# Routing the last sequence of a mixture-of-experts layer as a whole, with its small tiles in the attention's buffers

## The chip, the cores and the metric

The kernel runs on one core of one Trainium2 chip. The metric is the time of one execution on the device in microseconds (us), as the median of several runs; lower is better. The profile is that of one further execution, the profiled one, whose own time is given beside its span (first to last instruction). A core has five engines with a queue of instructions each: PE (TensorE, matrix products; PEld is its weight load), DVE (VectorE), ACT (ScalarE), POOL (GpSimd) and SP (SyncE, which here only issues transfers), and 16 DMA engines that all queues share.

## The reference, cut to what matters

The input x is 4 sequences of 1024 tokens with 256 features. Four layers follow one another, each added to x after a layer norm: a recurrent scan, a mixture of 8 experts (2 per token), a causal attention of 16 heads, and a mixture of 32 experts with 4 per token. The change is in the fourth:

```python
scores = jax.nn.sigmoid(X @ gate_w.T)
_, idx = jax.lax.top_k(scores + bias[None, :], K)            # K = 4 of E = 32
w = jnp.take_along_axis(scores, idx, axis=-1)
w = w / jnp.clip(jnp.sum(w, axis=-1, keepdims=True), 1e-12, None)
...
pos = jnp.take_along_axis(jnp.cumsum(onehot, axis=0) - 1, eid[:, None], axis=1)[:, 0]
valid = pos < C                                               # C = 256 places per expert
xe = jnp.zeros((E, C, D), x.dtype).at[eid, posc].add(jnp.where(valid[:, None], Xrep, ...))
h = jax.nn.silu(jnp.einsum('ecd,edi->eci', xe, W1)) * jnp.einsum('ecd,edi->eci', xe, W3)
ye = jnp.einsum('eci,eid->ecd', h, W2)
...
out = yrows.reshape(-1, K, D).sum(axis=1)
out = out + jax.nn.silu(X @ sw1.T) * (X @ sw3.T) @ sw2.T      # the shared expert
```

A place in an expert is given out in the order of the tokens, over all four sequences; who comes after the 256th gets none. So a token's place needs the counts of all tokens before it.

## The kernel before

x stays in SBUF as `x[b]`, one per sequence, [128, 8 tiles, 256 features and 7 further columns]: a tile is 128 tokens. The further columns carry mean, deviation and the slots of a token.

**Route** (`l4_route`, L920–1063) works on half a sequence, 4 tiles: mean and variance per tile (L927, L928), the reciprocal root in small steps on DVE (L895–912), the normalised rows `xn` (L934), their transposes on PE into `pt` (L946) and copies to `xT` by ACT (L950), the gate matmuls `pl` (L952–958, through `mm2`, L914, in two halves of 64 columns). Then on [128, 4 tiles x 32 experts]: score by Exp on ACT (L962) with an add and a reciprocal on DVE (L964, L965), score plus bias `selx` (L970), the best 8 per tile (L975, one instruction per tile), `match_replace` per tile (L980), `mask` (L982); a running count per expert, tile by tile (L986–993), which begins with the last count of the half before (`runs1`); the position of each token in each expert by matmuls `pos` (L998, L999); slot, free and their product (L1003–1007), the slots sorted per tile (L1010), the row numbers (L1013–1018). Each row goes to its slot in DRAM (`xs_d`) by an indirect DMA on POOL (`to_slots`, L874). In the last sequence only those of the best expert are sent at once, one per tile, so 4 per half; the others are kept in the list `late`, for a branch that is taken only when the lists overflow. After that come the shared expert's hidden rows (`s_l` matmuls, tanh L1040, L1041, L1043, each 128x512), the sum of the chosen scores (L1049–1053), and for each of the 4 choices three instructions that give `gates` (L1057, L1060, L1061). The function is a generator: its `yield` marks the places at which it may stop.

**Order of the work.** The attention is written out by hand under `manual_schedule` (`run_steps`), an order that the scheduler keeps. In its gaps `Beside` (L1571–1594) steps through a list of such generators, one piece at a time. Sequences 0 to 2 are routed that way, beside the next sequence's attention. After them comes `l4_experts_beside` (L1153–1245): the first list, up to 12 tiles of expert work, two by two. One round is: load of rows (`room`<-`xs_d`, SP, L1129) and weights (POOL, L1124), row numbers on DVE (L1134–1150), transposes `pta` (L1240), copy (L1242), matmuls `pea` (L918), tanh (L1227), two DVE products (L1228, L1229), matmuls `pya`, copy (L1212), and two scatters to `yt_d` (POOL, L874). What of it is left when the attention ends is done next. Then sequence 3 is routed, half after half:

```python
        drain(l3_out(B - 1, ps_s, "s"))
        while beside.jobs or beside.job is not None:
            beside.step()
        late = []
        for h in range(2):
            drain(l4_route(B - 1, h, sm, ps_s, "s", late))
```

Outside `manual_schedule` the scheduler orders each engine's queue and places waits; the order of issue above is only where it starts from.

**The end** (L1732–1895) opens new pools in the memory that the attention's pools gave back. In the order of the program: the total counts `pn` (L1780, L1781), `taken_b` (L1784), the list of the last 4 tiles (L1094–1114), the flag of an overflow (L1796–1800), 24 loads `yg` of expert results on SP (`l4_take`, L1747: 8 of 512 KB for sequence 0, with all four choices, and 16 of 128 KB for sequences 1 and 2, with the first), the last 4 tiles of expert work (`l4_tiles`: weights `ew` on POOL L1124, rows `xg` on SP L1129, L1134–1150, transposes `ptg` L1816, copy `xgT` L1818, `eh` L1825, `hid` L1830–1832, `ey` L1837, copy L1839, scatter to `yt_d`), the shared expert (`sy`, L1078), 48 adds of `yg` times gate into x (`l4_add`, L1756), stores of each half sequence on ACT's queue (L1774), and last the 8 loads `yg`, 8 adds and 2 stores of sequence 3.

Each DMA queue's completions are counted on 8 semaphores that the scheduler hands out in turn, to the loads of SP and the stores of ACT alike; a transfer waits for the one that had its semaphore before.

Of the kernel before, what the change touches and what calls it, by code (L numbers as in the profile page):

```python
# [57 lines left out]
def block_kernel(  # L58
# [861 lines left out]
    def l4_route(b, h, sm, ps, tag, late=None):  # L920

        nm = f"l4_{b}_{h}"
        HT = NT // 2
        half = slice(h * HT, (h + 1) * HT)
        for i in range(h * HT, (h + 1) * HT):
            st = l4s.tile([P, 6], F32, name=f"st_{nm}_{i}", tag="st1")
            nc.vector.bn_stats(st, x[b][:, i, :D])  # L927
            nc.vector.bn_aggr(x[b][:, i, D : D + 2], st)  # L928
            yield "dve"
        yield from rstd_pieces(x[b][:, half, D + 1], nm)  # L930
        xns = []
        for i in range(h * HT, (h + 1) * HT):
            xn = sm.tile([P, D], F32, name=f"xn_{nm}_{i}", tag="ln_xn", bufs=4)
            nc.vector.tensor_scalar(  # L934
                xn, x[b][:, i, :D], x[b][:, i, D : D + 1], x[b][:, i, D + 1 : D + 2],
                ALU.subtract, ALU.mult,
            )
            xns.append(xn)
            if i % 2:
                yield "dve"  # L940
        xT = l4s.tile([P, NC_, 512], F32, name=f"xT_{nm}", tag="xT1")
        for c in range(NC_):
            yield "pe"
            pt = ps.tile([P, 512], F32, name=f"pt_{nm}_{c}", tag=tag)
            for q in range(HT):
                nc.tensor.transpose(  # L946
                    pt[:, q * P : (q + 1) * P], xns[q][:, c * P : (c + 1) * P], ident
                )
            yield "post"
            nc.scalar.copy(xT[:, c, :], pt)  # L950
        yield "pe"
        pl = ps.tile([P, HT, E1], F32, name=f"pl_{nm}", tag=tag)  # L952
        for q in range(HT):
            for c in range(NC_):
                mm2(
                    pl[:, q, :], xT[:, c, q * P : (q + 1) * P], gate1_t[:, c, :],
                    c == 0, c == NC_ - 1,
                )
        yield "post"

        score = l4s.tile([P, HT, E1], F32, name=f"score_{nm}", tag="score")
        nc.scalar.activation(score, pl, AF.Exp, scale=-1.0)  # L962
        yield "dve"
        nc.vector.tensor_scalar(score, score, 1.0, None, ALU.add)  # L964
        nc.vector.reciprocal(score, score)  # L965
        yield "dve"

        selx = l4s.tile([P, HT, E1 + 8], F32, name=f"selx_{nm}", tag="selx")
        nc.vector.memset(selx[:, :, E1:], LOWEST)
        nc.vector.tensor_add(  # L970
            selx[:, :, :E1], score, bias1_t.unsqueeze(1).to_broadcast([P, HT, E1])
        )
        top = l4s.tile([P, HT, 8], F32, name=f"top_{nm}", tag="top1")
        for q in range(HT):
# [3 lines left out]
        rep = l4s.tile([P, HT, E1 + 8], F32, name=f"rep_{nm}", tag="rep1")  # L978
        for q in range(HT):
            nc.vector.match_replace(rep[:, q, :], top[:, q, :], selx[:, q, :], LOWEST)  # L980
        mask = l4s.tile([P, HT, E1], F32, name=f"mask_{nm}", tag="mask1")
        nc.vector.tensor_scalar(mask, rep[:, :, :E1], LOWEST, None, ALU.is_equal)  # L982
        yield "dve"


        run = l4s.tile([P, HT + 1, E1], F32, name=f"run_{nm}", tag="run1", bufs=2)  # L986
        if runs1:
            nc.vector.tensor_copy(run[:, 0, :], runs1[-1][:, HT, :])
        else:
            nc.vector.memset(run[:, 0, :], 0.0)  # L990
        runs1.append(run)
        for q in range(HT):
            nc.vector.tensor_add(run[:, q + 1, :], run[:, q, :], mask[:, q, :])
        yield "pe"
        pp = ps.tile([P, HT, E1], F32, name=f"pos_{nm}", tag=tag)
        for par in range(2):
            r = slice(par * DH, (par + 1) * DH)
            nc.tensor.matmul(pp[r], lower[:, r], mask, start=True, stop=False)  # L998
            nc.tensor.matmul(pp[r], ones[:, r], run[:, :HT, :], start=False, stop=True)  # L999
        yield "post"  # L1000

        slot = l4s.tile([P, HT, E1], F32, name=f"slot_{nm}", tag="slot1")
        nc.vector.tensor_add(slot, pp, slot1.unsqueeze(1).to_broadcast([P, HT, E1]))  # L1003
        free = l4s.tile([P, HT, E1], F32, name=f"free_{nm}", tag="free1")
# [3 lines left out]
        srt = l4s.tile([P, HT, 8], F32, name=f"srt_{nm}", tag="srt1")  # L1008
        for q in range(HT):
            nc.vector.max(srt[:, q, :], slot[:, q, :])  # L1010
        srt = srt[:, :, :K1]
        yield "dve"
        nc.vector.tensor_copy(x[b][:, half, D + 2 : D + 2 + K1], srt)  # L1013
        none = l4s.tile([P, HT, K1], F32, name=f"none_{nm}", tag="none1")
        nc.vector.tensor_scalar(none, srt, 0.0, float(NSLOT + 1), ALU.is_equal, ALU.mult)
        nc.vector.tensor_add(none, none, srt)
        row = l4s.tile([P, HT, K1], I32, name=f"row_{nm}", tag="row1", bufs=2)
        nc.vector.tensor_scalar(row, none, 1.0, None, ALU.subtract)
        for k in range(K1):
            for q in range(HT):  # L1020
                to = (row[:, q, k : k + 1], x[b][:, h * HT + q, :XP])
# [4 lines left out]
        nc.vector.tensor_reduce(  # L1026
            second[:, 2 * b + h : 2 * b + h + 1], srt[:, :, 1], AX.X, ALU.max
        )


        hid = l4s.tile([P, 512], F32, name=f"sh_{nm}", tag="shid", bufs=2)
        for w in (sw1_t, sw3_t):
            yield "pe"
            pt = ps.tile([P, 512], F32, name=f"s{0 if w is sw1_t else 1}_{nm}", tag=tag)
            for c in range(NC_):
                mm2(pt, w[:, c, :], xT[:, c, :], c == 0, c == NC_ - 1)
            yield "post"

            if w is sw1_t:
                nc.scalar.activation(hid, pt, AF.Tanh, scale=0.5)  # L1040
                nc.vector.scalar_tensor_tensor(hid, hid, 1.0, pt, ALU.add, ALU.mult)  # L1041
            else:
                nc.vector.scalar_tensor_tensor(hid, pt, 0.5, hid, ALU.mult, ALU.mult)  # L1043
        hid1[b, h] = hid


        yield "dve"
        gsum = l4s.tile([P, HT], F32, name=f"gsum_{nm}", tag="gsum1")
# [4 lines left out]
        nc.vector.tensor_mul(score, score, gsum.unsqueeze(2).to_broadcast([P, HT, E1]))  # L1053
        for k in range(K1):
            yield "dve"
            eq = l4s.tile([P, HT, E1], F32, name=f"eq_{nm}_{k}", tag="eq1")
            nc.vector.tensor_tensor(  # L1057
                eq, slot, srt[:, :, k : k + 1].to_broadcast([P, HT, E1]), ALU.is_equal
            )
            nc.vector.tensor_mul(eq, eq, score)  # L1060
            nc.vector.tensor_reduce(  # L1061
                gates1[:, b * NT + h * HT : b * NT + (h + 1) * HT, k], eq, AX.X, ALU.add
            )
# [89 lines left out]
    def l4_experts_beside(sm, ps, tag, w_of, ready):  # L1153
# [13 lines left out]
        for par in range(2):  # L1167
            r = slice(par * DH, (par + 1) * DH)
            nc.tensor.matmul(pn[r], ones[:, r], runs1[-1][:, NT // 2, :], start=True, stop=True)
# [108 lines left out]
    def drain(pieces):  # L1278
        for _ in pieces:
            pass  # L1280
# [4 lines left out]
    with ExitStack() as ph:  # L1285
# [320 lines left out]
        def run_steps():  # L1606
# [3 lines left out]
            for s in range(NU3 + 3):  # L1610
# [13 lines left out]
                if g == 2 and p == 0 and 0 < b < B:  # L1624
                    beside.jobs += [l4_route(b - 1, h, sm, ps_s, "s") for h in range(2)]
# [106 lines left out]
    with ExitStack() as ph:  # L1732
# [47 lines left out]
        nc.tensor.matmul(pn[:, :E1], ones, runs1[-1][:, NT // 2, :], start=True, stop=True)  # L1780
# [173 lines left out]
```

## Time and profile before

| what | value |
|---|---|
| median of 7 runs | 2041.05 us (2038.1 to 2047.75) |
| profiled execution, its own time | 2041.83 us |
| its span | 2040.1 us |
| mean granted TensorE clock | 0.956 |
| busy: PE, DVE, ACT, POOL | 1843.8, 1260.3, 961.2, 275.9 us |
| last matmul of the attention's output (`pz`) ends | 1946.4 us |
| score of the two halves of sequence 3 starts (ACT L962) | 1970.25 and 1984.25 us |
| first and last scatter of their rows start (POOL L874) | 1980.80 and 2000.82 us |
| first `yg` load, first `xg` load (SP) | 1981.61 and 2003.32 us |
| second `xg` op on DVE (L1134) | 2009.76 us |
| last output store issued | 2034.3 us |

Times in the trace count from the first instruction. A row of the timeline gives the start, the time in us, engine, line, operation, output<-input with partitions x elements, and how many instructions it puts together; in brackets the idle time before and what ended it. In a table of windows the granted clock is a share of the full one. The line of a helper (L918, L874) stands for all who call it, so the tile's name tells the step.

### The profile page before, as it was taken

The page shows a single profiled execution, that of the slowest core. Times are in us where ns is not written, and L with a number is a line of the kernel's source. Part 1 is how long each engine was busy: PE and PEld are TensorE (multiplying, and loading weights), DVE is VectorE, ACT ScalarE, POOL GpSimd, SP SyncE. Part 2 cuts the span into 40 slices and gives each one's busy share as a digit, 9 for nine tenths or more (in the row PEclk, how much of TensorE's full clock was granted, in tenths as well). Part 3 has the DMA queues.
Part 4 walks back from the last instruction along what each step waited for, and adds up shares of the span by engine and source line. Part 5 has one row for each costly group of instructions (what it writes and reads, how often), then busy time and mean ns, then how long its engine had stood idle before and what let it go on. Part 6 is the DMA issues. An engine that isn't in the chain of part 4 may idle for free.

```text
span 2040.1 us, 45193 instructions
## 1 busy us (share of the span) xinstructions
PE 1843.8 (90%) x17614; PEld 1204.6 (59%) x17614; DVE 1260.3 (62%) x4136; ACT 961.2 (47%) x2487; POOL 275.9 (14%) x307
## 2 busy tenths in 40 slices
PE   4688899999999999999999999998999999998864
PEld 2344466665666666666666666665566665666643
DVE  6576622244227776754677675577777477677667
ACT  3245322222236666663655655456565455655310
POOL 0333400022003200000003030000303003030122
PEclk8698999999999999999999999999999999999987
DMA  9111311122225433200000000000000000002127
GB/s 350 60 58 45 97 58 47 47 78 74 59 86 157 146 124 108 67 2 2 1 2 23 1 3 2 1 2 2 2 2 2 2 2 2 2 3 59 53 85 226
DMA packets 87151, 109.23 MB, mean 54 GB/s; under 512 B 13838, under 2 KB 76650, under 8 KB 85776
## 3 DMA queue, kind: packets, MB, share of 16 engines
q1 hardware_dynamic: 66528, 73.41, 11.0%
q0 software_dynamic: 15168, 27.05, 4.5%
q10 hardware_dynamic: 5232, 5.78, 0.8%
q8 instruction: 143, 2.34, 0.5%
q14 instruction: 80, 0.66, 0.1%
HBM read 51.75 MB, written 64.77 MB: 57 GB/s over the span
## 4 chain that ended last, share of the span: by engine, by line
PE 53%; DVE 12%; ACT 3%; issue 2%; DMA 1%; POOL 0%; SPq 0%; DVEq 0%; ACTq 0%; POOLq 0%
PE ps L1469 11%; PE pa L1555 9%; PE pt L1519 7%; PE pq L918 6%; PE pz L918 5%; PE pk L918 5%; PE pv L918 5%; DVE ps L1485 3%; ACT pe L1498 3%; PE s_l L918 1%; DVE pT L1540 1%; DVE nm L1483 1%; PE sy L918 1%; PE pb L1426 0%; DVE nm L1485 0%
## 5 line engine op out<-in xcount | busy, mean ns | idle before, releaser
L1498 ACT ACTIVATE pe<-ps,nm 128x512 f32<-128x512 f32 (+3 forms) x768 | 439.5, 579 | 286.9 <-DVE nm L1485 282.7
L1555 PE MATMUL pa<-pT,v 128*64 128x128 f32 (+1 forms) x4096 | 325.5, 292 | 0.0
L1555 PEld LDWEIGHTS pa<-pT,v 128*64 128x64 f32 x4096 | 244.0, 139 | 103.6 <-issue 85.3
L1469 PE MATMUL ps<-k,q 64*128 64x512 f32 (+3 forms) x1536 | 296.9, 502 | 0.0
L1519 PEld LDWEIGHTS pt<-ident,pe 64*128 64x128 f32 x4608 | 206.8, 141 | 114.6 <-issue 53.3
L1519 PE MATMUL pt<-ident,pe 64*128 64x64 f32 x4608 | 241.8, 230 | 28.3 <-ACT pe L1498 27.9
L609 PE MATMUL ph<-w_t,xgT 128*128 x544 | 256.7, 612 | 1.3 <-DVE hid L615 0.6
L1540 ACT COPY pT<-pt 128x512 f32<-128x512 f32 (+2 forms) x384 | 179.4, 521 | 164.8 <-PE pt L1519 163.1
L1483 DVE TENSOR_REDUCE nm<-ps 128x1 f32<-128x512 f32 x256 | 175.9, 687 | 124.2 <-PE ps L1469 123.1
L874 POOL DMA_INDIRECT xs_d<-x,row_l x104 | 103.2, 992 | 1038.8 <-DVE second L1026 988.2
L1540 DVE COPY pT<-pt 128x256 f32<-128x256 f32 (+3 forms) x384 | 178.1, 505 | 0.0
L1469 PEld LDWEIGHTS ps<-k,q 64*128 64x128 f32 x1536 | 134.6, 191 | 67.1 <-issue 54.8
L1485 DVE CUSTOM_DVE_ANT_0 ps<-ps,mask_a,nm 128x128 f32<-128x128 f32 (+3 forms) x256 | 143.1, 559 | 40.5 <-DVE nm L1483 9.2
L609 PEld LDWEIGHTS ph<-w_t,xgT 128*128 128x128 f32 x544 | 99.2, 195 | 101.2 <-issue 98.6
L1498 ACT ACTIVATION_READ_ACCUMULATOR pe<-ps,nm 128x1 f32 x768 | 152.2, 198 | 0.0
L918 PE MATMUL pq<-l_xT,w_pairs 128*64 128x512 f32 x448 | 113.2, 627 | 32.1 <-ACT pe L1498 32.1
L1485 DVE CUSTOM_DVE_ANT_0 ps<-ps,mask_a 128x128 f32<-128x128 f32 (+3 forms) x256 | 119.6, 517 | 24.3 <-PE ps L1469 22.0
L918 PE MATMUL pz<-wo_t,y 128*64 128x256 f32 x1024 | 115.0, 379 | 0.0
L918 PE MATMUL pv<-w_pairs,l_xT 128*64 128x128 f32 x1792 | 108.9, 274 | 2.9 <-ACT pe L1498 2.9
L629 PE MATMUL py<-w_t,hidT 128*128 x464 | 109.6, 379 | 0.0
L918 PE MATMUL pk<-l_xT,w_pairs 128*64 128x512 f32 x448 | 107.2, 599 | 0.0
L681 POOL DMA_INDIRECT yg<-yq_d,back x64 | 61.0, 953 | 306.0 <-issue 204.1
(422 smaller groups left out, 2243.8 us busy)
## 6 DMA issues: line engine op xcount, KB each, us to landing
yt_d<-zeros SPq DMA_DIRECT2D x32, 512.0 KB, 3.2
xg<-xe_d SPq DMA_DIRECT2D x68, 129.0 KB, 2.1
yq_d<-ys SPq DMA_DIRECT2D x68, 128.0 KB, 2.0
xs_d<-zeros SPq DMA_DIRECT2D x65, 131.5 KB, 2.6
w_t<-w_dram SPq DMA_DIRECT2D x8, 1024.0 KB, 13.2
w_pairs<-e_w_dram POOLq DMA_DIRECT2D x12, 384.0 KB, 3.5
x<-x_in_dram SPq DMA_DIRECT2D x8, 512.0 KB, 8.4
w_t<-w_dram SPq DMA_DIRECT2D x8, 512.0 KB, 13.6
```

Of the source, the lines that this page charges most:

```text
L609: nc.tensor.matmul(pt, xgT[:, c, :], w[:, c, k * H0 : (k + 1) * H0], start=(c == 0), stop=(c == NC_ - 1),)
L629: nc.tensor.matmul(py, hidT[:, c, :], w[:, c, :], start=(c == 0), stop=(c == H0 // P - 1))
L681: gather = nc.gpsimd.indirect_dma_start(out=yg, out_offset=None, in_=yq_d[: rows * P, :], in_offset=bass.IndirectOffsetOnAxis(ap=back_i[:, ...
L874: i = nc.gpsimd.indirect_dma_start(out=self.out, out_offset=bass.IndirectOffsetOnAxis(ap=idx, axis=0), in_=src, in_offset=None, bounds_che ...
L918: nc.tensor.matmul(out[r], lhsT[:, r], rhs, start=start, stop=stop)
L1469: nc.tensor.matmul(t[:, :n], qs[b, p][rows, i * P : (i + 1) * P], ks[b, p][rows, kc * 512 : kc * 512 + n], start=True, stop=True,)
L1483: nc.vector.tensor_reduce(m[:, 0:1], t, AX.X, ALU.min)
L1485: nc.vector.tensor_tensor_reduce(out=t[:, :n], in0=t[:, :n], in1=mask[:, 512 - n :], scale=1.0, scalar=-LOWEST if kc == 0 else m[:, 0:1], ...
L1498: inst = nc.scalar.activation(pe[:, :n], sps.pop((u, k, par))[:, :n], AF.Exp, bias=ms[u, i, par][:, 1:2], scale=-1.0, accum_out=ls[b, p][: ...
L1519: nc.tensor.transpose(pts[u][r][:, j, par, :], pes[u, k, par][rows, j * P : (j + 1) * P], ident[rows, rows],)
L1540: copy(to, pts[u][r][:, :n])
L1555: nc.tensor.matmul(pas[0][rows, cols], vs[b, p][:, j, rows], pTs[u][:, j, par, a * P :], start=(j == 0), stop=(j == nb - 1),)
```

## The change

`l4_route` takes a tuple `hs` of halves instead of one. Sequences 0 to 2 call it with one half, as before. For sequence 3 it is called once with both: norm, transposes and gate matmuls still go half by half, but the score and all that follows work on 8 tiles at once, 128x256 where it was 128x128; the instructions that go tile by tile (L975, L980, L993, L1010) stay as many. `xT` then comes from the pool that holds the attention's xT. The small tiles are packed, by the new inner function `new`, into `rooms`: three tiles of 128x1024 from the attention's pool `mid` with the tags q, k and v. The last running count is copied to a tile of its own, `end`, since `runs1` outlives the rooms. And the call is stepped in turn with what is left of the first list, one step of each, instead of after it.

```diff
-    def l4_route(b, h, sm, ps, tag, late=None):
+    def l4_route(b, hs, sm, ps, tag, late=None, rooms=None):
...
+        W = HT * len(hs)
+        T0 = hs[0] * HT
+        tiles = slice(T0, T0 + W)
+        if len(hs) > 1:
+            xT = xtp.tile([P, NC_, S], F32, name=f"xT_{nm}", tag="xT")
+        else:
+            xT = l4s.tile([P, NC_, 512], F32, name=f"xT_{nm}", tag="xT1")
+        at, kept = [0, 0], {}
+
+        def new(shape, name, tag, bufs=1):
+            if rooms is None:
+                return l4s.tile([P, *shape], F32, name=name, tag=tag, bufs=bufs)
+            if tag in kept:
+                return kept[tag]
+            n = shape[0] * (shape[1] if len(shape) > 1 else 1)
+            if at[1] + n > S:
+                at[:] = [at[0] + 1, 0]
+            v = rooms[at[0]][:, at[1] : at[1] + n]
+            at[1] += n
+            kept[tag] = v.rearrange("p (a b) -> p a b", b=shape[1]) if len(shape) > 1 else v
+            return kept[tag]
+
+        pl = None
+        for h in hs:
...
-        score = l4s.tile([P, HT, E1], F32, name=f"score_{nm}", tag="score")
+        score = new([W, E1], f"score_{nm}", "score")
...
-        runs1.append(run)
-        for q in range(HT):
+        for q in range(W):
             nc.vector.tensor_add(run[:, q + 1, :], run[:, q, :], mask[:, q, :])
+        end = run[:, W, :]
+        if rooms is not None:
+            end = l4s.tile([P, NL], F32, name=f"end_{nm}", tag="upto")[:, :E1]
+            nc.vector.tensor_copy(end, run[:, W, :])
+        runs1.append(end)
...
+        for h in hs:
+            c0 = h * 512 - T0 * P
+            hid = l4s.tile([P, 512], F32, name=f"sh_{nm}_{h}", tag="shid", bufs=2)
+            for w in (sw1_t, sw3_t):
...
         for k in range(K1):
             yield "dve"
-            eq = l4s.tile([P, HT, E1], F32, name=f"eq_{nm}_{k}", tag="eq1")
+            eq = new([W, E1], f"eq_{nm}_{k}", "eq1")
...
         drain(l3_out(B - 1, ps_s, "s"))
+
+        late = []
+        rooms = [mid.tile([P, S], F32, name=f"wide_{t}", tag=t) for t in ("q", "k", "v")]
+        for _ in l4_route(B - 1, (0, 1), sm, ps_s, "s", late, rooms):
+            beside.step()
         while beside.jobs or beside.job is not None:
             beside.step()
-        late = []
-        for h in range(2):
-            drain(l4_route(B - 1, h, sm, ps_s, "s", late))
```

The other lines of the diff replace `HT` by `W` and the tile pools by `new`, in the instructions named above.

More of the change, by code (lines that the diff above doesn't have):

```diff
@@ L918, in mm2 @@
             nc.tensor.matmul(out[r], lhsT[:, r], rhs, start=start, stop=stop)
-    def l4_route(b, h, sm, ps, tag, late=None):
-        nm = f"l4_{b}_{h}"
+    def l4_route(b, hs, sm, ps, tag, late=None, rooms=None):
+        nm = f"l4_{b}_{hs[0]}"
         HT = NT // 2
[L924 to L939, printed above, removed]
-                yield "dve"
-        xT = l4s.tile([P, NC_, 512], F32, name=f"xT_{nm}", tag="xT1")
-        for c in range(NC_):
-            yield "pe"
-            pt = ps.tile([P, 512], F32, name=f"pt_{nm}_{c}", tag=tag)
-            for q in range(HT):
[L946 to L958, printed above, removed]
@@ new lines, in l4_route @@
+        pl = None
+        for h in hs:
+            half = slice(h * HT, (h + 1) * HT)
+            for i in range(h * HT, (h + 1) * HT):
+                st = l4s.tile([P, 6], F32, name=f"st_{nm}_{i}", tag="st1")
+                nc.vector.bn_stats(st, x[b][:, i, :D])
+                nc.vector.bn_aggr(x[b][:, i, D : D + 2], st)
+                yield "dve"
+            yield from rstd_pieces(x[b][:, half, D + 1], f"{nm}_{h}")
+            xns = []
+            for i in range(h * HT, (h + 1) * HT):
+                xn = sm.tile([P, D], F32, name=f"xn_{nm}_{i}", tag="ln_xn", bufs=4)
+                nc.vector.tensor_scalar(
+                    xn, x[b][:, i, :D], x[b][:, i, D : D + 1], x[b][:, i, D + 1 : D + 2],
+                    ALU.subtract, ALU.mult,
+                )
+                xns.append(xn)
+                if i % 2:
+                    yield "dve"
+            c0 = (h - hs[0]) * 512
+            for c in range(NC_):
+                yield "pe"
+                pt = ps.tile([P, 512], F32, name=f"pt_{nm}_{h}_{c}", tag=tag)
+                for q in range(HT):
+                    nc.tensor.transpose(
+                        pt[:, q * P : (q + 1) * P], xns[q][:, c * P : (c + 1) * P], ident
+                    )
+                yield "post"
+                nc.scalar.copy(xT[:, c, c0 : c0 + 512], pt)
+            yield "pe"
+            if pl is None:
+                pl = ps.tile([P, W, E1], F32, name=f"pl_{nm}", tag=tag)
+            for q in range((h - hs[0]) * HT, (h - hs[0] + 1) * HT):
+                for c in range(NC_):
+                    mm2(
+                        pl[:, q, :], xT[:, c, q * P : (q + 1) * P], gate1_t[:, c, :],
+                        c == 0, c == NC_ - 1,
+                    )
@@ L966, in l4_route @@
         yield "dve"
-        selx = l4s.tile([P, HT, E1 + 8], F32, name=f"selx_{nm}", tag="selx")
+        selx = new([W, E1 + 8], f"selx_{nm}", "selx")
         nc.vector.memset(selx[:, :, E1:], LOWEST)
         nc.vector.tensor_add(
-            selx[:, :, :E1], score, bias1_t.unsqueeze(1).to_broadcast([P, HT, E1])
+            selx[:, :, :E1], score, bias1_t.unsqueeze(1).to_broadcast([P, W, E1])
         )
-        top = l4s.tile([P, HT, 8], F32, name=f"top_{nm}", tag="top1")
-        for q in range(HT):
+        top = new([W, 8], f"top_{nm}", "top1")
+        for q in range(W):
             nc.vector.max(top[:, q, :], selx[:, q, :E1])
@@ L977, in l4_route @@
         yield "dve"
-        rep = l4s.tile([P, HT, E1 + 8], F32, name=f"rep_{nm}", tag="rep1")
-        for q in range(HT):
+        rep = new([W, E1 + 8], f"rep_{nm}", "rep1")
+        for q in range(W):
             nc.vector.match_replace(rep[:, q, :], top[:, q, :], selx[:, q, :], LOWEST)
-        mask = l4s.tile([P, HT, E1], F32, name=f"mask_{nm}", tag="mask1")
+        mask = new([W, E1], f"mask_{nm}", "mask1")
         nc.vector.tensor_scalar(mask, rep[:, :, :E1], LOWEST, None, ALU.is_equal)
         yield "dve"
-        run = l4s.tile([P, HT + 1, E1], F32, name=f"run_{nm}", tag="run1", bufs=2)
+        run = new([W + 1, E1], f"run_{nm}", "run1", 2)
         if runs1:
-            nc.vector.tensor_copy(run[:, 0, :], runs1[-1][:, HT, :])
+            nc.vector.tensor_copy(run[:, 0, :], runs1[-1])
         else:
             nc.vector.memset(run[:, 0, :], 0.0)
-        runs1.append(run)
-        for q in range(HT):
+        for q in range(W):
             nc.vector.tensor_add(run[:, q + 1, :], run[:, q, :], mask[:, q, :])
+        end = run[:, W, :]
[3 more added lines that the diff above has]
+        runs1.append(end)
         yield "pe"
-        pp = ps.tile([P, HT, E1], F32, name=f"pos_{nm}", tag=tag)
+        pp = ps.tile([P, W, E1], F32, name=f"pos_{nm}", tag=tag)
         for par in range(2):
@@ L998, in l4_route @@
             nc.tensor.matmul(pp[r], lower[:, r], mask, start=True, stop=False)
-            nc.tensor.matmul(pp[r], ones[:, r], run[:, :HT, :], start=False, stop=True)
+            nc.tensor.matmul(pp[r], ones[:, r], run[:, :W, :], start=False, stop=True)
         yield "post"
-        slot = l4s.tile([P, HT, E1], F32, name=f"slot_{nm}", tag="slot1")
-        nc.vector.tensor_add(slot, pp, slot1.unsqueeze(1).to_broadcast([P, HT, E1]))
-        free = l4s.tile([P, HT, E1], F32, name=f"free_{nm}", tag="free1")
+        slot = new([W, E1], f"slot_{nm}", "slot1")
+        nc.vector.tensor_add(slot, pp, slot1.unsqueeze(1).to_broadcast([P, W, E1]))
+        free = new([W, E1], f"free_{nm}", "free1")
         nc.vector.scalar_tensor_tensor(free, pp, float(CAP), mask, ALU.is_lt, ALU.mult)
@@ L1007, in l4_route @@
         nc.vector.tensor_mul(slot, slot, free)
-        srt = l4s.tile([P, HT, 8], F32, name=f"srt_{nm}", tag="srt1")
-        for q in range(HT):
+        srt = new([W, 8], f"srt_{nm}", "srt1")
+        for q in range(W):
             nc.vector.max(srt[:, q, :], slot[:, q, :])
@@ L1012, in l4_route @@
         yield "dve"
-        nc.vector.tensor_copy(x[b][:, half, D + 2 : D + 2 + K1], srt)
-        none = l4s.tile([P, HT, K1], F32, name=f"none_{nm}", tag="none1")
+        nc.vector.tensor_copy(x[b][:, tiles, D + 2 : D + 2 + K1], srt)
+        none = new([W, K1], f"none_{nm}", "none1")
         nc.vector.tensor_scalar(none, srt, 0.0, float(NSLOT + 1), ALU.is_equal, ALU.mult)
         nc.vector.tensor_add(none, none, srt)
-        row = l4s.tile([P, HT, K1], I32, name=f"row_{nm}", tag="row1", bufs=2)
+        row = l4s.tile([P, W, K1], I32, name=f"row_{nm}", tag="row1", bufs=2)
         nc.vector.tensor_scalar(row, none, 1.0, None, ALU.subtract)
         for k in range(K1):
-            for q in range(HT):
-                to = (row[:, q, k : k + 1], x[b][:, h * HT + q, :XP])
+            for q in range(W):
+                to = (row[:, q, k : k + 1], x[b][:, T0 + q, :XP])
                 if late is not None and k > 0:
@@ L1025, in l4_route @@
                     to_slots(*to)
[L1026 to L1044, printed above, removed]
+        for h in hs:
+            nc.vector.tensor_reduce(
+                second[:, 2 * b + h : 2 * b + h + 1], srt[:, h * HT - T0 : (h + 1) * HT - T0, 1],
+                AX.X, ALU.max,
+            )
+        for h in hs:
+            c0 = h * 512 - T0 * P
+            hid = l4s.tile([P, 512], F32, name=f"sh_{nm}_{h}", tag="shid", bufs=2)
+            for w in (sw1_t, sw3_t):
+                yield "pe"
+                pt = ps.tile(
+                    [P, 512], F32, name=f"s{0 if w is sw1_t else 1}_{nm}_{h}", tag=tag
+                )
+                for c in range(NC_):
+                    mm2(pt, w[:, c, :], xT[:, c, c0 : c0 + 512], c == 0, c == NC_ - 1)
+                yield "post"
+                if w is sw1_t:
+                    nc.scalar.activation(hid, pt, AF.Tanh, scale=0.5)
+                    nc.vector.scalar_tensor_tensor(hid, hid, 1.0, pt, ALU.add, ALU.mult)
+                else:
+                    nc.vector.scalar_tensor_tensor(hid, pt, 0.5, hid, ALU.mult, ALU.mult)
+            hid1[b, h] = hid
         yield "dve"
-        gsum = l4s.tile([P, HT], F32, name=f"gsum_{nm}", tag="gsum1")
+        gsum = new([W], f"gsum_{nm}", "gsum1")
         nc.vector.tensor_mul(score, score, mask)
@@ L1052, in l4_route @@
         nc.vector.reciprocal(gsum, gsum)
-        nc.vector.tensor_mul(score, score, gsum.unsqueeze(2).to_broadcast([P, HT, E1]))
+        nc.vector.tensor_mul(score, score, gsum.unsqueeze(2).to_broadcast([P, W, E1]))
         for k in range(K1):
             yield "dve"
-            eq = l4s.tile([P, HT, E1], F32, name=f"eq_{nm}_{k}", tag="eq1")
+            eq = new([W, E1], f"eq_{nm}_{k}", "eq1")
             nc.vector.tensor_tensor(
-                eq, slot, srt[:, :, k : k + 1].to_broadcast([P, HT, E1]), ALU.is_equal
+                eq, slot, srt[:, :, k : k + 1].to_broadcast([P, W, E1]), ALU.is_equal
             )
@@ L1061, in l4_route @@
             nc.vector.tensor_reduce(
-                gates1[:, b * NT + h * HT : b * NT + (h + 1) * HT, k], eq, AX.X, ALU.add
+                gates1[:, b * NT + T0 : b * NT + T0 + W, k], eq, AX.X, ALU.add
             )
@@ L1168, in l4_experts_beside @@
             r = slice(par * DH, (par + 1) * DH)
-            nc.tensor.matmul(pn[r], ones[:, r], runs1[-1][:, NT // 2, :], start=True, stop=True)
+            nc.tensor.matmul(pn[r], ones[:, r], runs1[-1], start=True, stop=True)
         yield "post"
@@ L1624, in run_steps @@
                 if g == 2 and p == 0 and 0 < b < B:
-                    beside.jobs += [l4_route(b - 1, h, sm, ps_s, "s") for h in range(2)]
+                    beside.jobs += [l4_route(b - 1, (h,), sm, ps_s, "s") for h in range(2)]
                     beside.jobs += [l4_shared(b - 1, h, ps_s, "s") for h in range(2)]
@@ L1779, in block_kernel @@
         pn = ps_t.tile([P, E1 + 2 * B], F32, name="pn4", tag="t")
-        nc.tensor.matmul(pn[:, :E1], ones, runs1[-1][:, NT // 2, :], start=True, stop=True)
+        nc.tensor.matmul(pn[:, :E1], ones, runs1[-1], start=True, stop=True)
         nc.tensor.matmul(pn[:, E1:], ones, second, start=True, stop=True)
```

## The prediction, made before the changed kernel was run

> **What bounds the kernel now.** I read the page first (PE 90% busy), then the clock (0.956), the windows, the chain of waits, and SP's and VectorE's timelines. All lines are of the kernel before; its span is 2040.1 us, and the profiled execution took 2041.83, so 1.73 lie outside the span.
>
> The order listing of the two kernels shows every engine's work up to about 1951 us unchanged (but for two tiny VectorE instructions: a memset among the last attention's, in front of an instruction that waits for the same matmul and hides its 0.08, and a copy). PE sets the pace there, and nothing of it is touched. So only the last 90 us count. Windows (columns: stretch, length, busy PE, PEld, DVE, ACT, POOL with counts, granted clock, DMA share, GB/s):
>
> ```profile
> 1920.00:1940.00 20.00, 20.00 (x190) 13.29 (x188) 10.27 (x45) 0.00 (x0) 1.58 (x2) 1.00 0.12 35
> 1960.00:1980.00 20.00, 12.81 (x116) 8.32 (x114) 10.42 (x50) 3.66 (x8) 4.97 (x6) 0.83 0.06 19
> 1980.00:2000.00 20.00, 11.12 (x71) 6.86 (x68) 18.52 (x85) 1.95 (x4) 6.38 (x7) 0.74 0.85 305
> 2000.00:2020.00 20.00, 9.39 (x48) 8.53 (x48) 17.19 (x75) 3.35 (x11) 6.23 (x8) 0.66 0.63 187
> ```
>
> The reader is to see that after 1960 PE is no longer the bound. From 1980 on VectorE (18.5 of 20 us) and the DMA engines are both nearly full: the second half's route and the output's adds (L1756) run side by side. The chain of waits (start, length, what) names the last links:
>
> ```profile
> 2000.82 2.25 DMA xs_d<-x,row_l
> ...
> 2004.16 5.57 DMA xg<-xs_d
> 2009.73 0.03 issue
> 2009.76 0.41 DVE xg L1134
> 2010.17 0.08 DVE to_b L1148
> 2010.27 0.66 PE ptg L1816 x2
> 2010.93 1.71 PE eh L1825 x8
> ```
>
> So today the second half's last scatter, landed at 2003.07, releases the four last tiles; they then need 30.3 us from 2009.76 to the end. SP's queue, and what it waited for (total, times, longest):
>
> ```profile
> 1981.61 17.41 SPq L1747 DMA_DIRECT2D yg<-yt_d  x24
> 2003.32 3.53 SPq L1129 DMA_DIRECT2D xg<-xs_d  x4
> 2025.44 4.85 SPq L1747 DMA_DIRECT2D yg<-yt_d  x8
> ```
> ```profile
> SPq L1747 <- PE pt_l L946: 9.2, 1, 9.2
> ```
>
> The 24 yg loads (6.3 MB) stand ahead of the four xg loads. The first waits until the second half's transposes (1981.5) have read xn, because the yg tiles lie on the attention pools' memory.
>
> **What the change removes.** Every VectorE step from score to gates is done once at 128x256 instead of twice at 128x128:
>
> ```profile
> 1980.15 0.28 DVE L1057 TENSOR_TENSOR eq_l<-slot_l,srt_l 128x128 f32<-128x128 f32 x1
> 2000.15 0.42 DVE L1094 TENSOR_TENSOR eql<-key_b,entry 128x256 f32<-128x256 f32 x1
> 2003.00 4.04 DVE L1756 SCALAR_TENSOR_TENSOR x<-yg,gates,x 128x256 f32<-128x256 f32 x10
> ```
>
> A pair costs 2 x 0.285 = 0.57 before and 0.42 after. The 21 such pairs (nine in the route, twelve in the gates) save 21 x 0.15 = 3.2 us of busy VectorE; the max, match_replace and running-count instructions stay 8 each. Against this row stands the Trainium skill, Perfetto Trace Analysis, "Optimizing Scalar/DVE Operations": it gives about 60 ns of overhead per VectorE instruction on SBUF, and by that figure the saving would be 21 x 0.06 = 1.3 us, an estimate that the rest does not use.
>
> **What it moves: the score.** Norm, transposes (16, 1.10 us per 8) and gate matmuls (1.3 us per half) now lie between the left-over tiles' rounds. PE idles 1.37, 1.27 and 1.49 us per round there, waiting for VectorE's room, so most of it is covered. I add 1.0 to 1.5 us to the last pea's end (1964.53), then 14 of the gate matmuls (0.5). Score starts at about 1966.8, against 1970.25 and 1984.25 for the two halves. If the cover fails the whole 4.8 us of PE is paid: score at 1970.
>
> From score to mask: 0.3 for Exp (ACT), 0.36 add, 1.8 reciprocal (0.95 at half the width), 0.45 selx, 1.05 max x8, 0.1 memset, 1.5 match_replace x8, 0.37 mask: 5.9, so mask at about 1972.7.
>
> **What it adds: a wait.** The small tiles now lie in three of the attention's buffers, the memory where the yg tiles go. In the order listing the first yg load no longer waits for the transposes but for the *last* gates reduction (L1061). Behind it on SP stand 23 yg loads and the four xg loads, and behind those everything. From mask to that reduction: running counts with the gate sum between them 2.7; position matmuls 1.1 (the row before: count ended 1975.0, slot started 1976.76, with shared-expert matmuls between); slot, free, product, 8 max 2.1; the shared hidden's two 128x512 ops (0.69 each, now ahead of the row ids) 1.3; row ids and first gates 1.7; the second half's hidden 1.9; the taken list and three more gate steps of three 128x256 ops 3.7. Sum 14.5 at the pitch of back-to-back rows, 19 with full durations, PE at the half clock (0.50 granted between 1986 and 1994) and every wait counted. I take 16, nearest to the pitches since most of these ops are queued back to back: **first yg load at 1988.7** (1987 to 1992.5) instead of 1981.61: **+7.1**.
>
> **From the first yg load to the second xg op (L1134, 2009.76).** Before: 28.15 us. After, two lower limits. VectorE: first landing 4.1 us after the issue (1981.61 to 1985.69), then all 48 adds, which now stand ahead of the first xg op, at 0.40 = 19.3, then 1.0: 24.4. DMA: 6.3 MB yg, 1.6 ew, 0.3 xg and three to five output stores of 0.5 each = 9.7 to 10.7 MB at the 400 GB/s seen from 1984 to 1993, plus 2 of ramp: 26 to 29. The stores are nearer than they look: in the order listing the fifteenth yg load waits for the first store's landing (16 adds, then 3.6), and the third xg load for the third store's. I take 27.0 (bounds 24.4 and 29): **-1.15**. The scatters themselves end early: eight at 1.29 us from about 1981.5 land by 1994, not 2003.07, but nobody can use that while xg stands behind yg. POOL's order is unchanged: its eight scatters, then the four ew loads (1.6 MB), which wait for the list and so start some 10 us earlier, among the yg loads. On ACT the six output stores of the first three sequences now stand ahead of the xgT copies (L1818); the last store waits for the 48th add, as the first xg op does, so they cost nothing if VectorE is the limit and up to 2 us (six issues of 0.4) if they bunch, which the bound of 29 holds.
>
> The Trainium skill says in DMA: Bandwidth & Descriptors, "Rules for kernel authors": issue a DMA early and wait for it late. The change does the reverse for 6.3 MB. By the rule the whole 7 us would be lost; the rows say less, since VectorE needs 19.3 us for the adds in any case.
>
> **From there to the end.** Before 30.3 us. Now no adds stand between the tiles' steps: ey, which started at 2019.19 behind six adds, gains about 0.7. The last eight yg loads (first issue 2025.44, last landing 2032.55, 7.1 us for 1 MB) met output stores that are then done; at their 2.9 us shortest landing plus 2.6 for 1 MB they need about 5.5: 1.6 less. **-2.3** (0 to -3).
>
> **Sum.** +7.1 - 1.15 - 2.3 = +3.65. From the profiled execution's 2041.83 that is 2045.5; the median of the seven runs is 0.78 lower, so I forecast **2044.7** against 2041.05. Ends: 5.4 - 3.75 - 3 = -1.35 (2039.7) and 10.9 + 0.85 = +11.75 (2052.8).
>
> **Rivals.**
> - *Repaid whole.* VectorE's limit (24.4) holds instead of DMA's, and the tail gains all 3: about 2040.5. For it: 0.40 per add back to back, and score 17.5 us ahead of the second half's. Against: DMA near 400 GB/s for 9 us without a gap.
> - *Faster.* One mechanism, at SP's first yg load: the gates end early enough that adds and scatters both run ahead. Every term of the sum but the first is negative, so the point is a first load at 1985.1 for no change, and at 1981 for -0.2%; with the low ends (-6.75), 1984.3. The route would have to take 4 to 7 us less than the pitches say. Price then: 1982.0 - 1981.61 - 1.15 - 3 = -3.8, at best -6: about 2036.5.
> - *Worse.* The saturated DMA and the stores in the semaphores' turn decide: last gates at 1992.5, xg_1 at 29 to 31 after it, no gain in the tail: about 2052, up to 2056. For it: ew (1.6 MB) now falls among the yg loads, where before it came after them.
> - *It does not do what it says* (halves one after the other): the order listing shows 128x256 instructions, so almost excluded; 2041.
>
> **How the numbers follow.** A measurement of this kernel can tell about 0.2% (4.1 us) from no change: below 2037.0 and above 2045.1. Forecast's case (2041.5 to 2049) 0.50, split evenly by 2045.1: 0.25 and 0.25. Repaid 0.20: 0.17 within, 0.03 faster. Worse 0.18, slower. Faster 0.10. Nothing 0.02. So faster 0.13, same 0.44, slower 0.43. The range leaves out half of the faster case and about a third of the worse, and some of the repaid one: 2038 to 2053.
>
> **What would show it.** Right: a first yg load between 1987 and 1993 released by the gates reduction; score once at 128x256 near 1967; last scatter landed near 1994 and yet xg issued after 2008; 48 adds in a row; DMA share near 1 for 25 us; last yg loads in under 6 us. Wrong: a first yg load before 1985, or xg landing more than 29 us behind it.

## The result and the profile after

The changed kernel takes 2051.51 us in the median of 17 runs (2047.77 to 2057.63), the kernel before 2041.85 beside it (45 runs): the ratio is 1.0047, with a 95% interval of 1.0036 to 1.0058. It is slower by 9.7 us, which is more than the 0.2% that can be told from no change. The profiled execution took 2050.69 us with a span of 2048.9, against 2040.1 before; the granted clock is 0.953 against 0.956.

Until the attention's last `pz` matmul the two run alike (its end is at 1946.8, before at 1946.4). Everything else is in the tail behind it. The windows of the kernel after (columns as above):

```profile
1960.00:1980.00 20.00, 14.41 (x130) 9.39 (x128) 12.78 (x67) 3.75 (x8) 6.09 (x6) 0.83 0.06 19
1980.00:2000.00 20.00, 5.39 (x25) 2.78 (x21) 16.60 (x53) 0.89 (x2) 10.58 (x12) 0.72 0.51 176
2000.00:2020.00 20.00, 0.00 (x0) 0.00 (x0) 14.33 (x34) 0.00 (x0) 0.00 (x0) 0.50 1.05 356
2020.00:2040.00 20.00, 13.17 (x80) 9.88 (x80) 9.69 (x38) 3.99 (x12) 4.04 (x4) 0.84 0.30 90
```

From 2000 to 2020 PE, ACT and POOL compute nothing at all; VectorE and the DMA engines work alone. Before, PE had 9.39 us of tile work in that stretch. SP's queue of the kernel after:

```profile
1989.62 27.01 SPq L1785 DMA_DIRECT2D yg<-yt_d  x24
2017.43 3.42 SPq L1165 DMA_DIRECT2D xg<-xs_d  x4
2035.43 4.22 SPq L1785 DMA_DIRECT2D yg<-yt_d  x8
```

The 24 `yg` loads start 8.0 us later than before and take 27.01 us instead of 17.41, and the `xg` loads behind them are 14.1 later. (Before, SP stood 3.6 us for VectorE's flag, L1798, and 0.3 for the last scatter between the two; now the `xg` loads follow 0.8 us behind.) What SP waited for (total, times, longest):

```profile
SPq L1785 <- DVE gates L1097: 15.8, 1, 15.8
...
SPq L1785 <- DMA out_dram<-x: 4.5, 1, 4.5
```

The first wait is the one that the change brings, in front of the first load, in place of the 9.2 us for the transposes before. The second is in the middle of the loads: one of them waits 4.5 us for an output store of ACT's queue. The chain of waits shows both (start, length, what):

```profile
1989.07 0.43 DVE gates L1097
...
1989.62 3.71 DMA yg<-yt_d
...
1999.78 1.31 DVE x L1794 x4
2001.09 8.01 DMA out_dram<-x
2009.09 0.02 issue
2009.11 0.32 SPq L1785
...
2017.43 3.33 DMA xg<-xs_d
2020.76 0.03 issue
2020.79 0.42 DVE xg L1170
```

The chain no longer holds a scatter. It goes from the gates through the `yg` loads, 16 adds, the first output store, the other `yg` loads and only then to the tiles, whose rows had been in DRAM since about 1995: the last of the eight scatters started at 1992.40.

### The profile page after: what moved, and what is told of

Same layout as the page of the kernel before. It is cut to its first block, busy times and chain, and to the rows that moved or that the text cites. A ratio compares the mean times of both kernels' runs of the same rounds, so it can differ in the third digit from the quotient of the medians.

```text
span 2048.9 us, 45141 instructions
## 1 busy us (share of the span) xinstructions
PE 1840.3 (90%) x17606; PEld 1202.0 (59%) x17606; DVE 1261.4 (62%) x4106; ACT 961.2 (47%) x2486; POOL 274.7 (13%) x307
## 4 chain that ended last, share of the span: by engine, by line
PE 53%; DVE 12%; ACT 3%; issue 1%; DMA 1%; SPq 0%; DVEq 0%; ACTq 0%
PE ps L1505 10%; PE pa L1591 9%; PE pt L1555 7%; PE pq L918 6%; PE pz L918 5%; PE pk L918 5%; PE pv L918 5%; DVE ps L1521 3%; ACT pe L1534 3%; PE s_l L918 1%; DVE pT L1576 1%; DVE nm L1519 1%; PE sy L918 1%; DMA yg<-yt_d 1%; PE pb L1462 0%
```

## The experiments

**Theories.** A: the wait decides. The small tiles lie in rooms of the attention's pool, and SP's first `yg` load waits until that pool is given back; so the whole route of sequence 3 stands ahead of 6.3 MB of loads. Rivals: B, stepping the route in turn with the left-over tiles delays both; C, the loads lose their time in the middle, where loads of SP and stores of ACT take the same completion counts in turn; D, they lose it there because `ew` and the stores share the DMA engines with them.

The runs were on different chips: in the first and third group the kernel before took 2155.88 and 2150.91 us, in the second 2040.85. `after` was timed in full only in the first result, and e_keep only in the first and third group. So times are compared as ratios to the kernel before within a group, and profiles by the **tail**: us from the end of the last `pz` matmul to the start of an event, and to the end of the span.

| kernel | ratio to before, 95% | first `yg` | 24 loads take | first `xg` | last `yg` from | end |
|---|---|---|---|---|---|---|
| before | 1 | 35.2 | 17.4 | 56.9 | 79.1 | 93.7 |
| after | 1.0047 [1.0036, 1.0058] | 42.8 | 27.0 | 70.7 | 88.7 | 102.1 |
| e_keep | 0.9953 [0.9936, 0.9969] | 28.7 | 17.5 | 50.3 | 71.4 | 87.7 |
| e_turn_halves | 0.9997 [0.9978, 1.0016] | 38.1 | 17.6 | 57.2 | 82.1 | 96.6 |
| e_whole_after | 1.0070 [1.0049, 1.0091] | 50.5 | 26.8 | 78.5 | 96.4 | 111.2 |
| e_store_pool | 1.0028 [1.0010, 1.0047] | 44.2 | 22.5 | 68.0 | 88.5 | 103.3 |
| before_again | one run | 35.3 | 18.0 | 57.0 | 80.3 | 94.3 |
| after_again | one run | 42.8 | 27.3 | 71.4 | 89.0 | 103.8 |
| e_turn_again | 0.9977 [0.9960, 0.9994] | 31.3 | 17.3 | 49.3 | 72.9 | 87.5 |
| e_xg_first | 1.0021 [1.0005, 1.0036] | 42.8 | split | 48.4 | in one row | 97.0 |
| keep_again | 0.9959 [0.9942, 0.9976] | 28.5 | 18.0 | 50.2 | 71.3 | 87.4 |
| keep_pool | 0.9954 [0.9932, 0.9976] | 28.7 | 18.0 | 50.3 | 69.2 | 89.0 |
| keep_xg | 0.9955 [0.9937, 0.9973] | 29.4 | split | 50.7 | in one row | 88.8 |

**e_keep**: everything of the change stays, but the k and v tiles of the attention, in which the rooms now lie, come from a pool that is kept open to the end.

```diff
+        kv = ctx.enter_context(tc.tile_pool(name="l3_kv", bufs=2, side="right"))
...
-                    to[b, p] = mid.tile([P, S], F32, name=f"{nm}_{b}_{p}", tag=nm)
+                    to[b, p] = (kv if keys else mid).tile([P, S], F32, name=f"{nm}_{b}_{p}", tag=nm)
...
-                    vs[b, p] = mid.tile([P, NT, P], F32, name=f"v_{b}_{p}", tag="v")
+                    vs[b, p] = kv.tile([P, NT, P], F32, name=f"v_{b}_{p}", tag="v")
...
-        rooms = [mid.tile([P, S], F32, name=f"wide_{t}", tag=t) for t in ("q", "k", "v")]
+        rooms = [kv.tile([P, S], F32, name=f"wide_{i}", tag=t) for i, t in enumerate("vkv")]
```

> The changed kernel, but the attention's k and v tiles (tags k and v, 16 KB per partition) come from a pool of their own that stays open to the end, and the three rooms are taken from it. Nothing else is edited. Theory A (the wait): the first yg load waits for the last reader of the rooms because their pool is given back; with the rooms elsewhere it waits only for the last left-over tile (its matmuls end at 1968.8, its scatter, issued at 1971.2, lands at about 1973.4). So the first yg load at about 1973.5 instead of 1989.6, xg issued at 1992 to 1996 instead of 2017, and the end 14 to 20 us earlier: 2030 to 2036 for the median, under the kernel before too. Theory B (the work): the route in turns and at the whole width is what costs, and the loads are hidden either way: at most 3 us earlier than the changed kernel, 2048 to 2051. Theory C (the stores share semaphores with the loads, which holds back the fifteenth load by 4.5 us) alone: 5 us earlier, 2046.

Measured: 0.9953, that is faster than before by 0.5%, and by the two ratios, taken on two chips, some 19 us below after; the tails are 14.4 us apart. SP's queue, and its wait ahead of the first load, in e_keep:

```profile
2090.74 17.45 SPq L1786 DMA_DIRECT2D yg<-yt_d  x24
2112.34 2.85 SPq L1165 DMA_DIRECT2D xg<-xs_d  x4
2133.45 6.34 SPq L1786 DMA_DIRECT2D yg<-yt_d  x8
```
```profile
SPq L1786 <- DMA yt_d<-room,to_i_a: 18.0, 1, 18.0
```

The first load (28.7 us into the tail) now waits only for the left-over tiles' scatters, whose rows it reads; the wait for the gates is gone, and with it the 4.5 us wait for a store, since the loads are through before the gates let the adds run. The `xg` loads are now bound by the eight scatters, not by the `yg` loads. A is right, and it is worth more than the whole loss.

**e_turn_halves**: the turns alone, with the route half by half and no rooms.

```diff
-        rooms = [mid.tile([P, S], F32, name=f"wide_{t}", tag=t) for t in ("q", "k", "v")]
-        for _ in l4_route(B - 1, (0, 1), sm, ps_s, "s", late, rooms):
-            beside.step()
+        for h in range(2):
+            for _ in l4_route(B - 1, (h,), sm, ps_s, "s", late):
+                beside.step()
```

> The interleaving alone: sequence 3 is routed half after half with its tiles where the kernel before has them, but in turn with the first list's left-over tiles. Theory A: no room in the attention's pools, so the first yg load waits for the second half's transposes, which now come at about 1971, and for the last left-over scatter (1973.4): first yg load at about 1973.5, end 7 to 10 us below the kernel before, 2031 to 2035. Theory B (the turns cost): slower than the kernel before, 2043 to 2050.

Measured: 0.9997, no gain, where A had asked for 7 to 10 us. But its chain holds one 6.79 us wait of ACT's tanh L1263 of which the profile names no releaser ("another core or an unknown queue"), the only such wait in the tails of that chip, so the case was taken again below on another chip.

**e_whole_after**: the whole width alone; the route is drained after the left-over tiles.

```diff
-        for _ in l4_route(B - 1, (0, 1), sm, ps_s, "s", late, rooms):
-            beside.step()
         while beside.jobs or beside.job is not None:
             beside.step()
+        drain(l4_route(B - 1, (0, 1), sm, ps_s, "s", late, rooms))
```

> The whole width alone: sequence 3 is routed as a whole in the rooms, but after the left-over tiles, not in turn with them. Theory A: score some 5 us later than in the changed kernel (about 1972 against 1967.1), so the last gates and the first yg load 5 us later (1994 to 1995), and all behind it: 2055 to 2058. Theory B (the turns cost, not the wait): faster than the changed kernel, 2044 to 2049.

Measured: 1.0070, slower than after, though the intervals of the two ratios overlap; the tail ends at 111.2 against 102.1. SP's first wait in e_whole_after:

```profile
SPq L1784 <- DVE gates L1097: 23.8, 1, 23.8
```

Without the turns the gates are later and the wait is 8.0 us longer (23.8 against 15.8 in after). The turns save, they don't cost: B falls, and e_turn_again below bears it out.

**e_store_pool**: the six output stores of sequences 0 to 2 are issued from GpSimd (POOL), whose transfers have completion counts of their own.

```diff
-            nc.scalar.dma_start(out=out_view[b][:, half, :], in_=src[:, half, :D])
+            (nc.scalar if last is not None else nc.gpsimd).dma_start(
+                out=out_view[b][:, half, :], in_=src[:, half, :D]
+            )
```

> The changed kernel with the six output stores of sequences 0 to 2 issued from POOL instead of ACT, so that they no longer take turns with SP's loads on the same semaphores. Theory C (the semaphores): the 24 yg loads are issued in about 19 us instead of 27.0 and xg at about 2010 instead of 2017.4; end 5 to 7 us earlier, 2044 to 2047. Theory D (the 16 DMA engines are full, the stores cost their bytes wherever they are issued): the loads still take 25 to 27 us, within 2 us of the changed kernel, 2050 to 2053.

Measured: 1.0028, between the two. SP's queue in e_store_pool:

```profile
2099.27 22.49 SPq L1785 DMA_DIRECT2D yg<-yt_d  x24
2123.06 5.07 SPq L1165 DMA_DIRECT2D xg<-xs_d  x4
```

SP's waits list no store any more, and the 24 loads take 22.49 us: 4.5 less than after's 27.01, as much as the wait that has gone. The 5.1 us that remain over before's 17.41 fit D: `ew` (1.6 MB, 4 us at the 400 GB/s of the full stretches) still falls among the loads, as it doesn't in before and in e_keep; no run takes `ew` alone away. At the end little of it is seen: the tail of 103.3 us is no shorter than after's (102.1, and 103.8 below), the `xg` loads now meet five stores in a row and take 5.07 us instead of 3.42, and the intervals of this ratio and after's overlap. That C costs the loads 4.5 us is shown; that the end would gain as much is not.

**before_again and after_again**: both kernels unchanged on the second group's chip.

> The kernel before itself, profiled on the chip of this call, as the base for the stages of the other three. From the last pz matmul (the end of the attention's output) to the end of the span it should take 93 to 95 us, as in its first profile (93.7), whatever the time before it is on this chip.

> The changed kernel itself on the same chip. From the last pz matmul to the end 101 to 104 us (102.1 in its first profile); the first yg load 42 to 44 us after it, and the fifteenth yg load held up by the first output store again, so that the 24 loads take 26 to 28 us.

Measured: tails of 94.3 and 103.8, 9.5 apart, with the same waits (in after_again 15.9 us for the gates and 4.8 for the store). The tail's times carry over to this chip; on that of the first and third group neither of the two was profiled.

**e_turn_again**: the kernel of e_turn_halves on this chip.

> The interleaving alone once more. In its first profile ACT stood for 6.2 us in front of the last left-over tile's tanh, though the matmuls that it waits for are shown as done: releaser unknown. If that is a stall of that chip (such waits summed up to some 100 us over the kernel there, and there are none in the first two profiles), the tail falls from 96.6 to about 89 us here and the kernel is faster than before by 4 to 8 us. If it belongs to the kernel, the wait is there again and the time is that of the kernel before within 2 us.

Measured: 0.9977, by the ratio 4.7 us faster than before, with no unexplained wait; the tail ends at 87.5. (The end of the attention came late in this execution, at 1952.9, so its span alone shows no gain.) Its chain of waits shows what limits it now:

```profile
1998.10 11.48 DVE x L1794 x29
2009.58 0.33 DVE xg L1170
```

The rows of `xg` had their loads issued from 2002.12 on, but VectorE has the adds ahead of them. So the turns alone are worth about -5 us, and the whole width, as the change places its tiles, costs about +15 (e_whole_after): together about after's +10.

**e_xg_first**: the four `xg` and `ew` loads stand ahead of the 24 `yg` loads in the order of the program.

```diff
-        known = [(t, all_k if t < NT else first_k) for t in range((B - 1) * NT)]
-        ygs = [l4_take(*u) for u in known]
...
+        ahead = [l4_get(k, k, lst) for k in range(NL_B)]
+        known = [(t, all_k if t < NT else first_k) for t in range((B - 1) * NT)]
+        ygs = [l4_take(*u) for u in known]
...
-        l4_tiles(0, NL_B, lst)
+        l4_tiles(0, NL_B, lst, ahead)
```

> The changed kernel with the four xg and ew loads put ahead of the 24 yg loads in the program, rooms and turns as they are. Theory A with the queue (xg is late because it stands behind yg on SP): xg issued at about 48 us after the last pz matmul (last scatter 45.6, landing 2.3) instead of 70.7, the tile work falls among the adds, the stores come behind it on ACT, and the end is set by the 48 adds, which start 3 to 5 us later than in the changed kernel: tail 88 to 93 us against 102, so below the kernel before by 1 to 6 us. Theory D (full DMA engines set the end whatever the order): the tail stays within 3 us of the changed kernel's.

Measured: 1.0021, so a gain of about 5 us on after by the ratios, and 6.8 by the tails on this chip (97.0 against 103.8), but not the tail of 88 to 93 that was expected. SP's queue and the first of the four last scatters on POOL, in e_xg_first:

```profile
1985.87 0.81 SPq L1785 DMA_DIRECT2D yg<-yt_d  x2
1991.46 2.84 SPq L1165 DMA_DIRECT2D xg<-xs_d  x4
1994.36 36.73 SPq L1785 DMA_DIRECT2D yg<-yt_d  x30
```
```profile
2018.05 3.96 POOL L874 DMA_INDIRECT yt_d<-ys,to_i_b  x1 [25.81 <-DMA out_dram<-x]
```

The tiles come 22 us earlier into the tail (48.4 against 70.7), but their results then stand on POOL: the first scatter overwrites `yt_d`, which the 24 `yg` loads read, and in the program it waits for the counts of all of them; one of these again waited 4.7 us for a store. (The row names a store as what released it; the loads share their counts with the stores.) What was taken from one end of the queue is owed at the other.

**keep_again, keep_pool, keep_xg**: e_keep once more, with e_store_pool's edit, and with e_xg_first's.

> The kernel of e_keep once more, beside fresh runs of the kernel before. If the gain of e_keep (ratio 0.9953) is the changed release of the rooms and not something of the chip it ran on, the ratio is 0.992 to 0.997 again, the tail from the last pz matmul to the end 86 to 89 us beside some 94 of the kernel before, and the first yg load starts 28 to 30 us after the last pz matmul. If the chip's unexplained waits made part of the gain, the ratio is 0.997 to 1.0.

> The attention's k and v tiles in a pool of their own, and the six output stores of the first three sequences issued on GpSimd. In e_keep the 24 yg loads took 17.45 us already, and no yg load waited for a store, so theory C (stores and loads wait for each other through shared completion semaphores) expects nothing from the stores' move here: within 2 us of keep_again. If the stores' transfers or their issue on ScalarE still cost something at the end, it is 2 to 5 us below keep_again; if the four scatters to yt_d then stand behind the stores on GpSimd's queue, it is 2 to 6 us above.

> The attention's k and v tiles in a pool of their own, and the four xg loads ahead of the 24 yg loads in program order. With e_keep the xg loads wait for the eight scatters to xs_d, which end 50 us after the last pz matmul; on SyncE's queue the yg loads would then stand behind that wait, start 50 instead of 28.7 us after it, and hold back the scatters to yt_d, which overwrite what they read: 5 to 12 us above keep_again. If instead the adds in front of the xg operation on VectorE were what delays the tiles in keep_again, it is 1 to 5 us below.

Measured: 0.9959, 0.9954 and 0.9955, which no interval tells apart. e_keep's gain is confirmed. With the loads done before the first store, moving the stores gives nothing, as C says. For keep_xg both expectations missed, since the scheduler didn't put the `xg` loads first; SP's queue in keep_xg:

```profile
2083.61 13.82 SPq L1786 DMA_DIRECT2D yg<-yt_d  x16
2104.89 2.85 SPq L1165 DMA_DIRECT2D xg<-xs_d  x4
2107.80 23.75 SPq L1786 DMA_DIRECT2D yg<-yt_d  x16
```

16 `yg` loads still go ahead while the scatters run, and `xg` waits for the scatters 50 us into the tail, as in keep_again. Those eight scatters on POOL, 1.3 to 1.6 us apart once the slots are known, bind the best version: e_keep's chain of waits runs through them to the `xg` loads.

## Why the prediction was right in its direction and short in size

The forecast was 2044.7, slower by 3.65 us in a range of 2038 to 2053. The time lies in the range, near its upper end. By its own steps:

- **The score and the mask** held: score at 1967.10 (1966.8 forecast), the mask's end at 1972.9 (1972.7). The interleaving does hide the gate matmuls: without cover the forecast had the score at 1970.
- **The added wait** held: from the mask to the last gates 16.6 us (16 taken), first `yg` load at 1989.62 instead of 1988.7, +8.0 instead of +7.1, of which 0.4 is the later end of the attention. Its reason was wrong in part. The prediction says that the rooms lie in the memory where the `yg` tiles go. By the addresses in the built program they don't: the rooms are at 139 to 160 thousand bytes of a partition, the `yg` tiles at 70 to 120. The first load waits for the rooms' last reader all the same, so the wait goes by the memory given back and not by the load's own tile; e_keep, with the rooms in a pool that stays open and lies outside the new pool, takes it away. Whether the old pool as a whole counts, or all that the new pool spans (68 to 187 thousand bytes), no run tells apart.
- **From the first `yg` load to the second `xg` op** failed in size: 27.0 taken, bounds 24.4 and 29, and 32.2 measured (1989.62 to 2021.83), so +4.1 where -1.15 was forecast. This is the mis-sized term. The sum treated the stretch as 400 GB/s without a gap, for at most 10.7 MB. It did name the link that broke this, the fifteenth load that waits for the first store, but priced it at 16 adds and 3.6 us. The store was issued 11.5 us after the first load, and took 8.01 us to land, against a median of 3.6 among the DMA issues of before. Short windows of the kernel after show the stretch before its landing and the one behind it:

```profile
2001.00:2005.00 4.00, 0.00 (x0) 0.00 (x0) 3.44 (x9) 0.00 (x0) 0.00 (x0) 0.50 1.22 407
...
2009.00:2012.00 3.00, 0.00 (x0) 0.00 (x0) 2.83 (x8) 0.00 (x0) 0.00 (x0) 0.50 0.64 204
```

While the store was on its way the engines were full (share 1.22, 407 GB/s), with the loads and `ew`; when it had landed, the queue had run dry (0.64, 204 GB/s). The store took 4.4 us more than priced, but that is not what the wait cost the stretch. e_store_pool, where no load waits for a store, tells; windows of the whole stretch in after and in e_store_pool:

```profile
1989.62:2021.83 32.21, 0.53 (x2) 0.29 (x2) 23.66 (x66) 0.00 (x0) 5.28 (x7) 0.50 1.02 343
2099.27:2129.29 30.02, 0.66 (x2) 0.29 (x2) 23.29 (x66) 0.37 (x1) 9.85 (x13) 0.50 1.06 370
```

Time by rate, 11.0 and 11.1 MB were moved, more than the sum had allowed. At its own 400 GB/s and 2 us of ramp 11.0 MB take 29.6 us; without the wait the stretch took 30.0. So of the 5.2 us missed the bytes (`ew` and the stores among the loads) are about 3 and the wait for the store 2.2, by one profile of each kernel (after_again has 32.9).
- **The tail** held in sign and ended just past its far end (0 to -3): 27.1 us from the second `xg` op to the end against 30.3, -3.3 instead of -2.3. Of it 2.1 lie ahead of the last `yg` loads (0.7 forecast) and 1.2 behind their start (1.6 forecast).
- **Sum**: 8.0 + 4.1 - 3.3 = 8.8, as the spans differ. The second term came out above its bounds and the third below, so that the time stayed in the range is in part luck. One of the prediction's own signs of being wrong came true: `xg` landed 31.1 us behind the first `yg` load (1989.62 to 2020.76), where more than 29 was to count against it.
- **The 3.2 us of busy VectorE**, which the sum doesn't use, did not come. The wider instructions are as short as forecast (0.42 for L1093 at 128x256), but from the end of `pz` to the end of the span VectorE (the third busy time) is no less busy, before and after:

```profile
1946.40:2040.10 93.70, 47.96 (x384) 34.63 (x380) 64.40 (x268) 11.67 (x28) 23.91 (x26) 0.76 0.52 169
1946.80:2048.90 102.10, 44.30 (x376) 31.83 (x372) 65.75 (x238) 11.65 (x27) 23.94 (x26) 0.72 0.47 155
```

The forecast added up durations, and these overlap. In before L1005 starts 0.21 us after L1003, whose row says 0.29:

```profile
1976.76 0.29 DVE L1003 TENSOR_TENSOR slot_l<-pos_l,slot 128x128 f32<-128x128 f32 x1 [1.46 <-PE pos_l L999]
1976.97 0.28 DVE L1005 SCALAR_TENSOR_TENSOR free_l<-pos_l,mask_l 128x128 f32<-128x128 f32 x1
```

What the width alone saves, no run takes apart.
- **The rivals**: "worse" named the right mechanism for the middle (the stores in the semaphores' turn) and about the right time (2052), for partly wrong reasons: it wanted gates at 1992.5 and no gain in the tail, and its middle of 29 to 31 us was short of the 32.2. "Repaid whole" and "faster" asked for a middle of 24.4 to 27, which did not come.

The Trainium skill's rule, DMA: Bandwidth & Descriptors, "Rules for kernel authors", to issue a DMA early and wait for it late, was weighed with a loss of the whole 7 us. Here it was nearer than the sum: the loads start 8.0 later, the end is 8.8 later, and in e_keep, where by the tails they start 6.5 us earlier than before, the end is 6.0 earlier.

## What to carry to other kernels

Before a step borrows buffers from a pool that is about to be given back, look at who opens the next pool: here its first transfer waited for the borrower, and all that stands behind it on that queue waited too. The same change was worth +0.5% or -0.5% of time by nothing but the pool that its three tiles (with the attention's k and v) came from, each beside the kernel before on its own chip. Price a load that waits for a store at what the store takes among the loads around it, not at the median of a quieter stretch. And don't add up the durations of rows that overlap: compare busy times.

## What the runs showed of the hardware that was not expected

- A 512 KB store took 8.01 us to land among the loads; the median of before's stores was 3.6.
- PE had nothing to do for 34.7 us ahead of `ptg`, and the granted clock in the windows from 1989 to 2020 is 0.50.
- On the chip of the first and third group all kernels took 5% longer (2155.88 and 2150.91 against 2040.85 for the kernel before), with clocks of 0.93 instead of 0.955, and with waits whose releaser the profile doesn't know (one of 6.79 us in e_turn_halves). Why that is stays open; within a group it cancels, but for e_turn_halves, where it seems to have hidden the gain of e_turn_again.
